# Gate and up zeros: replicated by DMA instead of spread by a one-hot product

## The chip, the cores and the metric

One NeuronCore of a Trainium2 chip runs the whole kernel. It has five engines that run their own queues in order: PE (matrix products), DVE (VectorE), ACT (ScalarE), POOL (GpSimd) and SP (SyncE, which here only issues DMAs). They share SBUF, the on-chip memory of 128 partitions; products land in PSUM, of which each matmul output here takes one bank of 512 float32 per partition. The metric is the time of one execution on the device in microseconds (us). A profiled execution also leaves a trace, whose span begins with the first instruction and ends with the last.

## The reference

x has 1024 rows of 512. After a layer norm two branches are computed from the same xn: an attention with 32 heads (8 key and value heads), and a feed-forward block with quantised weights, whose output, through a SiLU, gates the attention. Only the feed-forward block matters for the change:

```python
def dequantize(imatrix, scales, zeros, group_size, out_dtype):
    rs = jnp.repeat(scales, group_size, axis=0)
    rz = jnp.repeat(zeros, group_size, axis=0)
    return ((imatrix.astype(rs.dtype) - rz.astype(rs.dtype)) * rs).astype(out_dtype)
gate_proj = dequantize(gate_w, gate_s, gate_z, GROUP_SIZE, dt)   # 512 x 1792, groups of 128 rows
up_proj = dequantize(up_w, up_s, up_z, GROUP_SIZE, dt)
down_proj = dequantize(down_w, down_s, down_z, GROUP_SIZE, dt)
gate = jax.nn.silu(jnp.dot(x, gate_proj))
up = jnp.dot(x, up_proj)
return jnp.dot(gate * up, down_proj)
...
x = x + s * g        # s: the attention of xn; g: silu of the feed-forward block of xn
```

Weights and zeros are integers from 0 to 15. A group is 128 input rows, so for each of the 4 groups (KT) every column has one zero and one scale.

## The kernel before

The kernel runs the feed-forward block first and the attention after it. The block's 1792 hidden columns are cut into 14 units (NI) of 128 columns. A unit holds its gate columns (m = 0) and its up columns (m = 1) side by side: integer weights of 128 partitions x 4 groups x 256 columns.

For each unit these steps are taken:

- gu_load (L228) brings the unit's integer weights into one of three buffers (tag "wi"), 512 KB.
- The zeros have to stand in all 128 partitions, since they are the same for all rows of a group. Three ways exist. gu_zeros (L222) once loads the zeros of all units, 14 rows of 1024, converts them to f16 (z16), and makes the one-hot matrices (pick). gu_spread (L237) then makes a unit's zeros in PSUM (z_ps) by two matmuls, each with the one-hot matrix that picks the unit's row and 512 of its columns; z_ps takes one of the four PSUM tiles that the products of the stage rotate through (pair, two banks each). gu_zeros_load (L244) brings them by one DMA that reads the unit's four rows of 256 numbers for each partition, into a row of h that is still free, as integers; units 1 and 2 use it, with the rows NI - 5 + it, that is 10 and 11.
- gu_subtract (L250) takes weights minus zeros on DVE and writes f16 (guq, three buffers). All products of the unit read guq.
- gu_unit (L312) multiplies. xn is held as a sum of two f16 parts (xth, xtl), so each product is two matmuls. Units 0 to 2 are done in two halves of 512 rows (tb = 0, 1), units 3 to 13 in one go (tb is None): for each m and each group j, four matmuls of 512 columns into one pair.
- gu_scaled (L258) takes a pair out of PSUM with the group's scale: groups 0 and 2 by ACT (L273), groups 1 and 3 by DVE, which adds onto what ACT wrote (L275). The two sums that arise are added by POOL (gu_total, L295). The Silu is ACT's (L299), and gate times up goes into the unit's row of h (gu_h, L305): by POOL for odd units, by DVE for even ones and for the halves.

h (L209) is 14 rows of 1024 numbers in each partition; row it belongs to unit it. Rows 12 and 13 first hold half of x (ln_load), rows 10 and 11 the zeros of units 1 and 2.

The order of the work on every engine is written out by hand: instructions stand on each engine in the order of the Python code. A unit's gate and h, which are late, are done in the next unit (gu_finish, lists in behind), after its first group for m = 0 and for m = 1. In the same way unit it, after its first group, prepares unit it + 1: it spreads the zeros (L357; L317 for the halves), subtracts (L358), and issues the weight load of unit it + 4 (L360, gu_load(subtract + 3)), into the buffer that the subtract has just freed. Behind that weight load on SP stands one of the loads of the first projection weights (L803, wide).

Around the stage: ln_* make xth and xtl; unit 10 is followed by a few small products for the first projection (norms, L590 and L595 on DVE), and in units 12 and 13 the first down weights are prepared (dn_dequant L491, whose L493 and L494 are a difference and a product; split_r L143, whose L147 is a difference; all of them with both inputs in SBUF). The down stage (L826) follows, then the attention.

Of the kernel before, what the change touches and what calls it, by code (L numbers as in the profile page):

```python
# [15 lines left out]
I32 = mybir.dt.int32  # L16
# [14 lines left out]
NI = FF // P  # L31
NT = S // P
HT = NT // 2
KT = DM // P
# [75 lines left out]
def attention_gated_by_ffn_kernel(ctx, tc, x, gu_w, gu_z, gu_s, dn_w, dn_z, dn_s, wq, wkv, wo, qnw, knw, out):  # L110
# [98 lines left out]
    h = fp.tile([P, NI, S], F32, name="h")  # L209
# [3 lines left out]
    def pair(name):  # L213
        return fpsum.tile([P, 2, 512], F32, tag="pair", name=name)
# [13 lines left out]
    def gu_load(it):  # L228
        wi = gp.tile([P, KT, 256], I32, tag="wi", name=f"gui{it}", bufs=3)
        if it:  # L230
            sp.dma_start(wi, gu_w[it])
        else:
            for m in range(2):
                sp.dma_start(wi[:, :, m * P : m * P + P], gu_w[it][:, :, m * P : m * P + P])
        gu_raw[it] = wi

    def gu_spread(it):  # L237

        ps = pair(f"z_ps{it}")
        for k in range(2):  # L240
            te.matmul(ps[:, k, :], lhsT=pick[:, it, :], rhs=z16[:, k * 512 : k * 512 + 512], start=True, stop=True)
        gu_raw[it, "z"] = ps.rearrange("p a c -> p (a c)").rearrange("p (k c) -> p k c", k=KT)

    def gu_zeros_load(it):  # L244

        zb = h[:, NI - 5 + it, :].bitcast(I32).rearrange("p (k c) -> p k c", k=KT)
        sp.dma_start(zb, gu_z[:, it].partition_broadcast(P))
        gu_raw[it, "z"] = zb

    def gu_subtract(it, m=None):  # L250
        if it not in gu_int:
            gu_int[it] = gp.tile([P, KT, 256], F16, tag="wq", name=f"guq{it}", bufs=3)
        c = slice(0, 256) if m is None else slice(m * P, m * P + P)
        ve.tensor_tensor(gu_int[it][:, :, c], gu_raw[it][:, :, c], gu_raw[it, "z"][:, :, c], ALU.subtract)
# [3 lines left out]
    def gu_scaled(unit, m, j, ps):  # L258

        it, tb = unit  # L260
        w = ps.shape[1]
        if j == 0:
            if tb is None or m == 0:
                tag = m if tb is None else (it + tb + 1) % 2
                two = gu_sums[unit, "tile"] = gp.tile([P, 2, S], F32, tag=("gs", "us")[tag], name=f"g{m}_{it}_{tb}")
            else:
                two = gu_sums[unit, "tile"][:, :, 512:]
            for i in range(2):
                gu_sums[unit, m, 2 * i] = two[:, i, :w]
        a = gu_sums[unit, m, j - j % 2]  # L270
        scale = gsT[:, it, m, j : j + 1]
        if j % 2 == 0:
            se.activation(a, ps, AF.Copy, scale=scale)  # L273
        else:
            ve.scalar_tensor_tensor(a, ps, scale, a, ALU.mult, ALU.add)  # L275

    def gu_first(m, banks):

        two = gp.tile([P, 2, S], F32, tag=("gs", "us")[m], name=f"g{m}_first")
        parts = [two[:, 0, :512], two[:, 1, :512], two[:, 0, 512:]]  # L280
        for j, a in enumerate(parts):
            se.activation(a, banks[j], AF.Copy, scale=gsT[:, 0, m, j : j + 1])
        gu_sums[(0, 0), m, 0] = parts[0]

        def rest():
            a, b, c = parts
            ve.scalar_tensor_tensor(c, banks[3], gsT[:, 0, m, 3:4], c, ALU.mult, ALU.add)
            ge.tensor_tensor(a, a, b, ALU.add)
            ge.tensor_tensor(a, a, c, ALU.add)

        return rest

    def gu_total(unit, m):
        a = gu_sums[unit, m, 0]
        ge.tensor_tensor(a, a, gu_sums.pop((unit, m, 2)), ALU.add)  # L295
# [11 lines left out]
    def gu_finish(k):  # L307

        if behind[k]:
            (gu_gate, gu_h)[k](behind[k].pop(0))  # L310

    def gu_unit(it, tb, subtract=None, first=False, halfway=lambda rest: None, finish=True, meanwhile=lambda: None, total=True):  # L312
        unit = (it, tb)
        w = gu_int[it]
        rest = []
        if subtract is not None and tb is not None:
            gu_spread(subtract)  # L317
        for m in range(2):
            ws = slice(m * P, m * P + P)
            banks = {}  # L320
            for j in range(KT):
                if tb is None:
                    banks[j] = pair(f"gu_ps{it}_{m}_{j}")
                    for x in (xth, xtl):
                        for k in range(2):
                            te.matmul(
                                banks[j][:, k, :], lhsT=w[:, j, ws], rhs=x[:, j, k * 512 : k * 512 + 512], start=x is xth, stop=x is xtl
                            )
                    banks[j] = banks[j].rearrange("p a c -> p (a c)")
                else:  # L330
                    if j % 2 == 0:
                        both = pair(f"gu_ps{it}_{tb}_{m}_{j}")
                    banks[j] = both[:, j % 2, :]
                    if not (first and m == 0):
                        for x in (xth, xtl):
                            te.matmul(
                                banks[j], lhsT=w[:, j, ws], rhs=x[:, j, tb * 512 : tb * 512 + 512], start=x is xth, stop=x is xtl
                            )
                    elif j == KT - 1:
                        for c in (0, 256):  # L340
                            for x in (xth, xtl):
                                for i in range(KT):
                                    te.matmul(
                                        banks[i][:, c : c + 256], lhsT=w[:, i, ws], rhs=x[:, i, c : c + 256], start=x is xth, stop=x is xtl
                                    )
                if tb is None:
                    gu_scaled(unit, m, j, banks[j])
                elif j % 2 and not first:
                    for i in (j - 1, j):
                        gu_scaled(unit, m, i, banks[i])  # L350
                if j == 0 and finish and tb is None:
                    gu_finish(m)
                    if total and m == 1:
                        gu_total(unit, 0)
                if m == 0 and j == (1 if tb is not None else 0) and subtract is not None:
                    if tb is None:
                        gu_spread(subtract)  # L357
                    gu_subtract(subtract)  # L358
                    if subtract + 3 < NI:
                        gu_load(subtract + 3)  # L360
                if m == 0 and j == 1 and tb is None:
                    meanwhile()
            if first:
                rest.append(gu_first(m, banks))
            elif total and not (tb is None and m == 0):
                gu_total(unit, m)
            for _ in range(finish if tb is not None else 0):
                gu_finish(m)
            if m == 0:
                halfway(rest)  # L370
        for k in range(2):
            behind[k].append(unit)
        return rest
# [53 lines left out]
    for t in range(HT, NT):  # L427
        ln_load(t)
    gu_load(1)
    gu_zeros_load(1)  # L430
    gu_load(2)
    gu_zeros_load(2)

    warm = pair("warm")[:, 0, :]
# [14 lines left out]
        ln_split(t)  # L449
    for it in (3, 4, 5):  # L450
        gu_load(it)

    def other_rows(rest):

        for t in range(HT, NT):
            ln_stats(t)
            if t > HT:
                ln_moments(t - 1)
        ln_moments(NT - 1)
        ln_rstd(1, lambda: gu_subtract(1))  # L460
        for t in range(HT, NT):
            ln_norm(t)
        rest.pop(0)()
        gu_subtract(2)

    for f in gu_unit(0, 0, first=True, finish=False, halfway=other_rows):
        f()
    gu_unit(1, 0, finish=False)
    for t in range(HT, NT):
        ln_transpose(t)  # L470
        ln_split(t)
    gu_unit(2, 0, finish=2)
    gu_unit(0, 1, finish=1)
    gu_unit(1, 1, finish=1)
# [351 lines left out]
    for it in range(NI):  # L826
        for tb in range(2):
# [14 lines left out]
            for i in range(4):  # L842
                c = slice(i * P, i * P + P)
# [529 lines left out]
```

## Time and profile before

| what | us |
|---|---|
| median of three runs | 1022.02 |
| lowest and highest of them | 1018.25, 1023.63 |
| the profiled execution | 1020.44 |
| its span in the trace | 1018.6 |
| PE busy in the span | 964.7 (95%) |
| DVE busy | 857.2 (84%) |
| ACT busy | 775.5 (76%) |
| POOL busy | 429.4 (42%) |
| units 0 to 2 (halves) begin, units 3 to 13 begin, down stage begins | 13.1, 45.2, 130.7 |

Shares over the whole span are means over stages with different limits: POOL, at 42% of the span, is busy for 67 of the 85.5 us of the units 3 to 13. The instructions that make and use the zeros, by the view of the lines:

```profile
L241 PE MATMUL z_ps<-z,pick x24: 374/379/385, 7.9 to 115.3; 14*128 14x512 f16 x24
L254 DVE TENSOR_TENSOR guq<-gui,z_ps x13: 679/1210/1221, 8.5 to 115.8; 128x1024 f16<-128x1024 int32 x11, 128x512 f16<-128x512 int32 x2
```

The columns are line, engine, operation, count, the shortest, middle and longest duration in ns, and the first and last start in us. A matmul's recorded duration is longer than the distance to the next one's start, because matmuls overlap in the array; costs on PE are therefore read from starts.

### The profile page before, as it was taken

How to read it: one execution, taken by the hardware profiler on the slowest of the kernel's cores; microseconds unless marked ns; L12 is line 12 of the kernel's file. 1: busy time of each engine (PE TensorE's matmuls, PEld its weight loads, DVE VectorE, ACT ScalarE, POOL GpSimd, SP SyncE). 2: the span in 40 equal slices, each digit the busy share in tenths (PEclk: the TensorE clock that was granted, in tenths of full speed). 3: DMA queues.
4: the chain of work that ended last, by engine and by line, in shares of the span. 5: the costliest groups of instructions: out<-in, count | busy, mean ns of one | idle time of the engine just before them, and what ended most of it. 6: DMA issues, size and time to landing. Idle time of an engine off the chain costs nothing. (4 is left out here: it accounts for less than half of the span.)

```text
span 1018.6 us, 17980 instructions
## 1 busy us (share of the span) xinstructions
PE 964.7 (95%) x5688; PEld 561.8 (55%) x5688; DVE 857.2 (84%) x1764; ACT 775.5 (76%) x2160; POOL 429.4 (42%) x424
## 2 busy tenths in 40 slices
PE   6899999999999999996998999999999999989995
PEld 4344477854444444444555666665676666656562
DVE  7888998728888878877898998987989989969985
ACT  5777745778878887787887987987879978858861
POOL 2588764216666555564235151051241421530722
PEclk9999999999999999999999999999999999999999
DMA  7132359535998999998898999997999999999994
GB/s 251 37 121 93 104 170 310 187 125 163 204 273 190 245 229 215 236 237 202 172 196 161 206 216 183 227 203 158 231 202 191 212 201 190 202 219 198 218 201 108
DMA packets 425063, 195.74 MB, mean 192 GB/s; under 512 B 371522, under 2 KB 382078, under 8 KB 424958
## 3 DMA queue, kind: packets, MB, share of 16 engines
q1 hardware_dynamic: 424958, 194.50, 85.5%
q8 instruction: 46, 0.75, 0.3%
q14 instruction: 59, 0.48, 0.1%
HBM read 76.27 MB, written 27.27 MB: 102 GB/s over the span
## 5 line engine op out<-in xcount | busy, mean ns | idle before, releaser
L1074 DVE SCALAR_TENSOR_TENSOR p<-pf,row,p 128x384 f16<-128x384 f32 (+7 forms) x256 | 208.8, 816 | 20.9 <-ACT p L1066 18.0
L1047 ACT ACTIVATE pf<-pf,row 128x384 f32<-128x384 f32 (+7 forms) x256 | 184.9, 723 | 41.6 <-DVE row L1041 37.3
L1041 DVE CUSTOM_DVE_ANT_0 pf<-s,trel,cs 128x384 f32<-128x384 f32 (+7 forms) x256 | 191.4, 748 | 19.8 <-PE s L153 19.7
L1066 ACT ACTIVATE p<-pf,row 128x384 f16<-128x384 f32 (+7 forms) x256 | 184.0, 719 | 6.3 <-DMA pT<-p 1.4
L151 PE MATMUL s<-kT,qT 128*128 128x512 f16 (+3 forms) x356 | 115.3, 324 | 11.8 <-DVE row L1041 11.5
L994 POOL TENSOR_SCALAR wl<-wl,rvs 128x512 f32<-128x512 f32 x32 | 53.7, 1677 | 149.0 <-DMA wl<-in_wo 130.0
L152 PE MATMUL s<-kT,qT 128*128 128x512 f16 (+3 forms) x356 | 115.4, 324 | 0.0
L153 PE MATMUL s<-kT,qT 128*128 128x512 f16 (+3 forms) x356 | 114.0, 325 | 0.0
L716 POOL TENSOR_TENSOR f<-f,inv 128x512 f32<-128x512 f32 (+1 forms) x96 | 102.1, 1084 | 1.4
L151 PE MATMUL m<-v,wh 128*128 128x512 f16 x248 | 95.0, 383 | 0.0
L153 PE MATMUL m<-v,wh 128*128 128x512 f16 x248 | 94.9, 383 | 0.0
L151 PE MATMUL o<-pT,vT 128*128 128x256 f16 (+1 forms) x302 | 79.6, 264 | 13.9 <-DMA pT<-p 13.7
L151 PEld LDWEIGHTS <-vT 128*128 128x128 f16 x594 | 58.9, 99 | 57.8 <-DMA pT<-p 15.1
L1110 ACT ACTIVATE wh<-o 128x256 f16<-128x256 f32 x128 | 47.7, 373 | 54.4 <-PE o L153 53.8
L152 PEld LDWEIGHTS <-vT 128*128 128x128 f16 x594 | 58.9, 99 | 41.4 <-issue 4.5
L152 PE MATMUL o<-pT,vT 128*128 128x256 f16 (+1 forms) x302 | 79.6, 264 | 0.0
L153 PE MATMUL o<-pT,vT 128*128 128x256 f16 (+1 forms) x302 | 79.3, 264 | 0.0
L151 PE MATMUL o<-wide,vT 128*128 128x256 f16 (+1 forms) x292 | 75.9, 260 | 3.1 <-DMA wide<-p 3.1
L152 PE MATMUL o<-wide,vT 128*128 128x256 f16 (+1 forms) x292 | 75.9, 260 | 0.0
L153 PE MATMUL o<-wide,vT 128*128 128x256 f16 (+1 forms) x292 | 75.7, 260 | 0.0
L151 PE MATMUL m<-wh,xth 128*128 128x512 f16 x192 | 72.8, 379 | 1.2 <-ACT h L869 1.2
L153 PE MATMUL m<-wh,xtl 128*128 128x512 f16 x192 | 72.8, 379 | 0.0
(200 smaller groups left out, 2531.4 us busy)
## 6 DMA issues: line engine op xcount, KB each, us to landing
qd<-tr SPq DMA_DIRECT2D x48, 256.0 KB, 3.3
qT<-qd SPq DMA_DIRECT2D x24, 512.0 KB, 4.4
wide<-in_wq SPq DMA_DIRECT2D x32, 256.0 KB, 3.7
wo_sq<-in_wo SPq DMA_DIRECT2D x8, 1024.0 KB, 7.8
wl<-in_wo SPq DMA_DIRECT2D x32, 256.0 KB, 3.6
gui<-in_gu_w SPq DMA_DIRECT2D x13, 512.0 KB, 3.7
wide<-in_wkv SPq DMA_DIRECT2D x16, 256.0 KB, 3.8
vd<-v SPq DMA_DIRECT2D x8, 512.0 KB, 4.7
```

The lines of the kernel that those rows point to most:

```text
L151: te.matmul(ps, lhsT=lh, rhs=rh, start=first, stop=False)
L152: te.matmul(ps, lhsT=lh, rhs=rl, start=False, stop=False)
L153: te.matmul(ps, lhsT=ll, rhs=rh, start=False, stop=last)
L716: ge.tensor_tensor(f, f, ib, ALU.mult)
L994: ge.tensor_scalar(wor[g, i], wor[g, i], rvs[:, g : g + 1], None, ALU.mult)
L1041: ve.tensor_tensor_reduce(p, ps, trel[g][:, S - w :], cs[:, hh : hh + 1], 3e38, ALU.add, ALU.min, least[:, c])
L1047: se.activation(p, p, AF.Exp, bias=least[:, c], scale=-1.0, accum_out=total[:, c])
L1066: se.activation(p16[u, qt][:, :, 0, :], pf[u, qt], AF.Copy, scale=scale[:, qt : qt + 1])
L1074: ve.scalar_tensor_tensor(lo, p, scale, hi, ALU.mult, ALU.subtract)
L1110: se.activation(oh, av_ps[u], AF.Copy, scale=1.0 / P_SCALE)
```

## The change

The zeros of units 3 to 13 no longer come from products. gu_zeros_load now serves every unit but the first, into the unit's own row of h from unit 3 on, and the spreads in gu_unit go. The loads for units 3 to 5 stand behind their weight loads at the beginning, those for units 6 to 13 behind the weight load of the same unit. gu_subtract is the same line as before, but its second input, for units 3 to 13, is h in SBUF in place of z_ps in PSUM. Unit 0 keeps its spread.

```diff
     def gu_zeros_load(it):
 
-        zb = h[:, NI - 5 + it, :].bitcast(I32).rearrange("p (k c) -> p k c", k=KT)
+        row = NI - 5 + it if it < 3 else it
+        zb = h[:, row, :].bitcast(I32).rearrange("p (k c) -> p k c", k=KT)
         sp.dma_start(zb, gu_z[:, it].partition_broadcast(P))
         gu_raw[it, "z"] = zb
...
         rest = []
-        if subtract is not None and tb is not None:
-            gu_spread(subtract)
         for m in range(2):
...
                 if m == 0 and j == (1 if tb is not None else 0) and subtract is not None:
-                    if tb is None:
-                        gu_spread(subtract)
                     gu_subtract(subtract)
                     if subtract + 3 < NI:
                         gu_load(subtract + 3)
+                        gu_zeros_load(subtract + 3)
...
     for it in (3, 4, 5):
         gu_load(it)
+        gu_zeros_load(it)
```

## The prediction

> **What bounds the kernel now.** I read three views, in this order: the busy time of the engines over the gate and up stage (its units 3 to 13 run from 45.2 to 130.7 us), the timeline of one pair of units in it, and the timeline wherever VectorE (DVE) and GpSimd (POOL) meet.
>
> ```profile
> core 0: us, PE busy (x) PEld busy (x) DVE busy (x) ACT busy (x) POOL busy (x), PEclk, DMA share, GB/s
> 45.20:130.70 85.50, 83.56 (x378) 35.02 (x378) 77.55 (x69) 61.90 (x64) 67.08 (x28) 1.00 0.33 106
> ```
>
> Of 85.5 us PE is busy 83.6, DVE 77.6 and POOL 67.1: PE sets the pace, at full clock (1.00), and DVE stands only 10% behind. DMA is busy a third of the time.
>
> ```profile
> 60.76 0.59 PE L326 MATMUL gu_ps<-xtl,guq 128*128 128x512 f16 x2
> 61.29 0.60 PE L241 MATMUL z_ps<-z,pick 14*128 14x512 f16 x2
> 61.82 0.61 PE L326 MATMUL gu_ps<-xth,guq 128*128 128x512 f16 x2
> ```
>
> Columns, here and below: start, duration, engine, line, operation. This is PE around one spread, L241. The spreads of units 4, 5 and 6 start at 53.74, 61.29 and 68.83: a unit takes 7.55 us, a pair 15.09, and PE has no gap in between. The other two engines in the same pair:
>
> ```profile
> 54.63 2.36 POOL L295 TENSOR_TENSOR g_None<-g_None 128x1024 f32<-128x1024 f32 x1 [0.50 <-DVE g_None L275]
> 57.07 2.36 POOL L305 TENSOR_TENSOR h<-g_None 128x1024 f32<-128x1024 f32 x1
> 59.40 2.35 POOL L295 TENSOR_TENSOR g_None<-g_None 128x1024 f32<-128x1024 f32 x1
> 62.18 2.37 POOL L295 TENSOR_TENSOR g_None<-g_None 128x1024 f32<-128x1024 f32 x1 [0.43 <-DVE g_None L275]
> 66.34 3.21 POOL L295 TENSOR_TENSOR g_None<-g_None 128x1024 f32<-128x1024 f32 x1 [1.79 <-DVE g_None L275]
> ```
>
> ```profile
> 62.02 1.21 DVE L254 TENSOR_TENSOR guq<-gui,z_ps 128x1024 f16<-128x1024 int32 x1
> ...
> 66.11 1.22 DVE L305 TENSOR_TENSOR h<-g_None 128x1024 f32<-128x1024 f32 x1
> ```
>
> An even unit (4, from 54.47, its subtract, on) has three POOL instructions: the second total of the unit before (L295), an odd unit's h (L305), its own first total (L295). An odd unit (5, from 62.02 on) has two, and DVE makes the even unit's h (66.11). POOL's L295 takes 2.37 us beside the subtract L254, but 3.21 us beside DVE's h.
>
> ```profile
> 21.44 1.22 DVE L254 TENSOR_TENSOR guq<-gui,h 128x1024 f16<-128x1024 int32 x1
> ...
> 21.67 2.11 POOL L289 TENSOR_TENSOR g_first<-g_first 128x512 f32<-128x512 f32 x1 [3.75 <-DVE g_first L287]
> ...
> 118.42 2.68 POOL L305 TENSOR_TENSOR h<-g_None 128x1024 f32<-128x1024 f32 x1
> ...
> 118.93 2.72 DVE L494 TENSOR_TENSOR dni<-dni,dns 128x512 f32<-128x512 f32 x1
> ...
> 138.45 1.11 DVE L147 TENSOR_TENSOR dnl<-dni,dnh 128x512 fp32r<-128x512 f32 x1 [1.84 <-ACT dnh L145]
> ...
> 138.97 2.85 POOL L295 TENSOR_TENSOR g_None<-g_None 128x1024 f32<-128x1024 f32 x1
> ```
>
> The first two rows are the future form of the subtract, with zeros from h in SBUF (units 1 and 2 have it already): POOL's 512-wide sum, 1.28 us two rows later (23.73), takes 2.11, because it gets going only when the subtract is over (22.66). The next two are the reverse: a DVE product of two SBUF tiles (this width takes 0.68 us undisturbed, as at 144.02) ends at 121.65, 0.55 after POOL's h (121.10). So a DVE instruction with both inputs in SBUF and a POOL instruction exclude each other, and the one that comes second waits for the other's end. With one input in PSUM they don't: beside the subtract at 62.02 POOL kept its 2.37. The last two show who comes next when both wait: a POOL instruction ended at 139.01 with the next one ready, and DVE's 138.45 still ended at 139.56, 0.55 after the first, while POOL's next was stretched to 2.85. DVE gets in between.
>
> **What the change removes.** Eleven spreads (L241, two matmuls and two weight loads each). The price of one: the group before it starts its last pair at 60.76, the next group would start 0.43 later, at 61.19, and starts at 61.82: 0.63 us. Eleven are 6.9 us of PE, and PE's pair would fall from 15.09 to 13.83. It also takes z_ps out of the four PSUM pairs, which lets PE run a pair further ahead.
>
> **What it adds on the queues.** Eleven loads of 512 KB through SP, each some 0.65 us to issue (this load's own rows for units 1 and 2: 0.66 and 0.63). They stand behind the weight load of the same unit and ahead of a wide<-in_wkv or wide<-in_wq load, which then goes out 0.65 later and is read first at 98.4. The zeros of unit 6 go out near 45.6 and are read at 62.0. This load's own two landings took 8.3 and 9.3 us (in the first 20 us, where the DMA share is 0.80; in the stage it is 0.33), so some 7 us of cover are left; I take 0. Without the cover a late landing would hold DVE's subtract and, one unit later, PE, by what it is late. The rows of h that are used are written by their own unit much later and wait for nothing.
>
> **What it moves: the subtract onto POOL's port.** Its duration stays (1.21 with z_ps, 1.21 to 1.22 with h). But it now excludes POOL, ten times in this stretch. I work out a pair by hand from the rows. A DVE 1024-wide instruction that has waited ends 1.08 after POOL's end (1.21 less the 0.13 by which the 512-wide 0.68 exceeds 0.55). A POOL 1024-wide one that has waited ends 2.22 after DVE's end (66.34+3.21 against 66.11+1.22). DVE starts its next instruction 1.13 after a subtract, 1.2 after an L275.
>
> Even unit, from its subtract at 0, which starts 0.16 ahead of POOL's total as at 62.02 and 62.18: subtract to 1.21, POOL's second total to 3.43, h to 5.87 (back to back, 2.44 as 57.07 to 59.40 and neighbours), first total to 8.19. DVE meanwhile needs only 1.13 and four times L275: it wants its next subtract at about 6.8 and finds POOL in flight until 8.19. That subtract ends at 9.27, as if it had started at 8.06. Even unit: 8.06.
>
> Odd unit, from there: subtract to 1.21, POOL's total to 3.43. DVE: L275 at 1.13, a second at 2.4 (ScalarE's Silu had to wait for the total that ended 0.13 into the unit), DVE's h at 3.6 to 4.84, POOL's first total waits and ends at 7.06, L275 at 4.75 and 5.94, next subtract at 7.12, just after POOL is through. Odd unit: 7.12.
>
> The pair: 15.18 against 15.09 now. Put as a sum: five POOL instructions of 2.36 (11.8) and three DVE ones of 1.08 that exclude them (3.25) are 15.05, and POOL now has no idle time left to pay with. So what PE gives up is taken by the port between DVE and POOL; five pairs cost +0.5 instead of -6.3.
>
> The edges: the unit 2 subtract at 43.96 meets a POOL sum that ends at 44.31: +0.23, given back by the spread that went before it. In unit 11 two small DVE reads (L590, L595) stand ahead of the subtract, so that POOL's total (now ready at about 108.05, after an h that waits for Silu as now) goes first and the subtract ends at 111.5 instead of 109.3; the next one is at 117.3 instead of 115.8. In unit 12 the wait of L494 (2.04 of its 2.72) is given back: L493 and L494 follow each other while POOL is held, and the L275 behind them starts at 121.85 against 121.57. At 126.7 L147 finds POOL's last total in flight until 128.8 (now 127.66). The down stage begins 1.1 us later than 130.67. From there PE is busy (19.9 of 20 us in 140 to 160) and the shift goes through to the end. **Sum:** +1.2 us; bounds of the unknown part -6.9 (the exclusion costs nothing) and +11.5 (below). On the profiled execution, 1020.44 us with a span of 1018.6, that is 1021.6; the median of the three runs is 1022.02, so the forecast is 1023.2.
>
> One rule of the Trainium skill speaks for the opposite: Perfetto Trace Analysis, Optimization Strategies, makes it the goal to keep the matmul engine used and to work on whatever blocks it. By it, 6.9 us taken off a PE that waits for nobody would be 6.9 us gained, a time of 1015.1, against 1023.2 by the rows; the rows at 21.44 and 21.67 are why I don't follow it.
>
> **Rivals.** (1) PE stays the bound and the 6.9 us come out: 1015.1. For it: POOL is idle 2.4 us a pair today, DVE 1.8, PE not at all. Against it: the pair would have to shrink by 1.26 and hold two more exclusions of 1.08, which is 3.4 us out of POOL's 2.4. (2) The port goes to the wrong one: when the even unit's first total ends, POOL's second total, long ready, goes ahead of the waiting subtract (8.19 to 10.53). DVE's subtract, and with it h and the rest of the odd unit, comes 2.3 later: the pair is 17.5, five pairs +11.5, 1033.5. It decides above 0.5% from three pairs of five on (2.3 x 3 = 6.9). Against it is 138.45 to 139.56; for it, that the margin by which the subtract leads POOL's total elsewhere is only 0.16 us, which unit 11 loses. (3) The zeros land late, or the change moves no PE time at all: the first needs a landing over 16 us, the second is excluded by the 22 matmuls that the built program no longer has.
>
> **Chances.** What a measurement of this kernel can tell from no change is about 0.5%, 5.1 us. The forecast (a change between -4 and +5 us): 0.60. Rival 1, or most of it: 0.10. Beyond +5: 0.30, half of it rival 2 at most pairs, half single lost margins of about 2 us each, three or more of them. So faster 0.10, same 0.60, slower 0.30. The forecast's own range is 1019 to 1027; to leave out no more than two in ten I take 1018 to 1030.
>
> **What would show it.** Right: L254 stands at 1.2 in some units and 2 to 3 us in others, alternating; POOL's L295 mean rises from 2.55 to about 3; PE shows waits for DVE of about 1.3 us a pair where it had 0.63 of spread; pairs of subtracts stay 15.1 to 15.2 apart. Wrong: pairs of 13.9 (rival 1), or of 17.5 with DVE waiting through two POOL instructions (rival 2). A first matmul of a unit that waits for a DMA of in_gu_z would be rival 3.

## The result and the profile after

| | us |
|---|---|
| changed kernel, median of 22 runs | 1022.68 (1018.8 to 1026.4) |
| kernel before, median of 22 runs beside them | 1019.87 (1015.03 to 1023.63) |
| ratio of the two | 1.0031, 95% interval 1.0018 to 1.0044 |
| profiled execution of the changed kernel, and its span | 1018.8, 1016.9 |
| first and last start of a matmul of the down stage, before | 130.67, 208.81 |
| the same, changed | 133.77, 211.63 |

By the ratio, the change made the kernel slower by about 3.2 us (1.8 to 4.5), which lies inside the 0.5% that the forecast counted as no change. The predicted 1023.2 lies 0.5 from the measured 1022.68, but part of that is luck: the kernel before measured 1019.87 beside it and not the 1022.02 that the forecast started from. To be compared with the forecast's +1.2 is the +3.2. The profiled execution of the changed kernel is the quickest of its 22 runs, and the one of the kernel before is slower than its median; so the two traces are compared interval by interval and not by their spans.

Line numbers of the changed kernel are one higher than before's from the subtract (L255) to h (L306): L276 is DVE's accumulation, L274 ACT's copy, L296 POOL's total, L300 the Silu. First the engines in units 3 to 13, in the kernel before and in the changed one (busy us and, in brackets, instructions of PE, PEld, DVE, ACT and POOL, then clock, DMA share and GB/s):

```profile
core 0: us, PE busy (x) PEld busy (x) DVE busy (x) ACT busy (x) POOL busy (x), PEclk, DMA share, GB/s
45.00:131.00 86.00, 83.98 (x379) 35.28 (x379) 78.05 (x70) 62.40 (x66) 67.15 (x28) 1.00 0.33 106
...
45.00:131.00 86.00, 77.00 (x355) 34.36 (x354) 82.85 (x67) 60.61 (x65) 75.25 (x28) 1.00 0.46 153
```

PE lost the 7 us of the spreads, as the change meant it to, and DVE went from 78.05 to 82.85 of 86 us, POOL from 67.15 to 75.25. The waits of the same stretch (total us, times, longest) tell who is waited for, first a row of the kernel before, then the same of the changed one:

```profile
PE gu_ps L326 <- DVE g_None L275: 1.5, 3, 1.1
...
PE gu_ps L325 <- DVE g_None L276: 7.5, 6, 3.0
```

PE's waits for DVE's accumulations were 1.5 us before and are 7.5 now: the time that the spreads left went there, 6.0 of it. Now one pair of units (start, duration, engine, line, operation). A subtract stands one unit ahead of the unit whose weights it makes: "unit 3's subtract" makes unit 3's weights and stands in unit 2; "the even unit's subtract" stands in an even unit.

```profile
72.42 1.21 DVE L255 TENSOR_TENSOR guq<-gui,h 128x1024 f16<-128x1024 int32 x1
72.58 3.28 POOL L296 TENSOR_TENSOR g_None<-g_None 128x1024 f32<-128x1024 f32 x1 [0.24 <-DVE g_None L276]
...
78.25 5.65 POOL L296 TENSOR_TENSOR g_None<-g_None 128x1024 f32<-128x1024 f32 x2
...
79.02 2.66 DVE L255 TENSOR_TENSOR guq<-gui,h 128x1024 f16<-128x1024 int32 x1
...
83.99 1.21 DVE L306 TENSOR_TENSOR h<-g_None 128x1024 f32<-128x1024 f32 x1
...
87.51 1.21 DVE L255 TENSOR_TENSOR guq<-gui,h 128x1024 f16<-128x1024 int32 x1
```

The even unit's subtract (72.42) goes first, and POOL's total beside it, 2.37 in the kernel before, takes 3.28. The odd unit's subtract (79.02) finds POOL in flight, takes 2.66, and stretches the two totals of POOL's row at 78.25 to 5.65 (4.7 without it). From 72.42 to 87.51 the pair is 15.09, what it was before (15.16, 15.09 and 15.10), and so are its neighbours (57.33, 72.42, 87.51, 102.60). The pairs gained nothing and lost nothing. What the trace shows as lost lies at the two ends of the stage. Its start, in the kernel before and in the changed one:

```profile
43.96 1.21 DVE L254 TENSOR_TENSOR guq<-gui,z_ps 128x1024 f16<-128x1024 int32 x1
...
54.47 1.21 DVE L254 TENSOR_TENSOR guq<-gui,z_ps 128x1024 f16<-128x1024 int32 x1
```

```profile
43.16 2.95 POOL L296 TENSOR_TENSOR g<-g 128x512 f32<-128x512 f32 x2 [0.33 <-DVE g L276]
...
45.56 1.64 DVE L255 TENSOR_TENSOR guq<-gui,h 128x1024 f16<-128x1024 int32 x1
...
48.00 2.95 POOL L296 TENSOR_TENSOR g<-g 128x512 f32<-128x512 f32 x2 [1.89 <-DVE g L276]
...
49.75 2.29 DVE L255 TENSOR_TENSOR guq<-gui,h 128x1024 f16<-128x1024 int32 x1
...
57.33 1.21 DVE L255 TENSOR_TENSOR guq<-gui,h 128x1024 f16<-128x1024 int32 x1
```

The subtracts of units 3 and 4 (45.56, 49.75), which took 1.21 before, take 1.64 and 2.29, each behind one of POOL's 512-wide totals. The stage's end, again before and changed:

```profile
118.14 0.75 DVE L493 TENSOR_TENSOR dni<-dni,dnz 128x512 f32<-128x512 int32 x1
...
122.90 0.59 PE L326 MATMUL gu_ps<-xth,guq 128*128 128x512 f16 x2 [1.12 <-DVE g_None L275]
```

```profile
108.42 5.67 POOL L296 TENSOR_TENSOR g_None<-g_None 128x1024 f32<-128x1024 f32 x2
...
110.66 1.22 DVE L255 TENSOR_TENSOR guq<-gui,h 128x1024 f16<-128x1024 int32 x1
...
118.18 3.27 POOL L296 TENSOR_TENSOR g_None<-g_None 128x1024 f32<-128x1024 f32 x1 [0.24 <-DVE g_None L276]
...
120.35 1.66 DVE L492 TENSOR_TENSOR dni<-dni,dnz 128x512 f32<-128x512 int32 x1
...
121.53 2.68 POOL L306 TENSOR_TENSOR h<-g_None 128x1024 f32<-128x1024 f32 x1
122.04 2.71 DVE L493 TENSOR_TENSOR dni<-dni,dns 128x512 f32<-128x512 f32 x1
...
126.00 0.59 PE L325 MATMUL gu_ps<-xth,guq 128*128 128x512 f16 x2 [2.95 <-DVE g_None L276]
```

In unit 11 the subtract (110.66, unit 12's) kept its 1.22. In unit 12 the first down-weight subtract (120.35), which was 0.75 before, finds POOL's stretched total of 118.18 in flight and takes 1.66, and DVE's next one still waits for POOL's h (121.53), as before. The accumulations behind them are late by that much, and PE waits 2.95 us for one of them where it waited 1.12.

Read from these two executions, interval by interval:

| interval | before | changed | difference |
|---|---|---|---|
| unit 3's subtract to unit 5's | 10.51 | 11.77 | +1.26 |
| unit 5's to unit 11's | 45.35 | 45.27 | -0.08 |
| unit 11's to unit 13's | 16.00 | 15.42 | -0.58 |
| unit 13's to the first matmul of the down stage | 14.85 | 15.75 | +0.90 |
| sum | 86.71 | 88.21 | +1.50 |

The other 1.6 of the 3.1 us that the table shows at the down stage's start were there ahead of unit 3's subtract (45.56 against 43.96). I put them down to this execution and not to the change: its granted clock over the first 43 us is 0.92 where before's is 1.00, two windows of 3.4 us in which PE had half its clock, and the first of them began at 12.1, ahead of the first load that the change adds (13.16). Three kernels below had two such windows there as well (45.53, 44.73 and, with the second window twice as long, 46.91; the first of the three has none of the added loads); in those without a window this subtract stands at 43.8 to 44.6, with the loads or without.

### The profile page after: what moved, and what is told of

Same layout as the page of the kernel before. It is cut to its first block, busy times and chain, and to the rows that moved or that the text cites. A ratio compares the mean times of both kernels' runs of the same rounds, so it can differ in the third digit from the quotient of the medians.

```text
span 1016.9 us, 17949 instructions
## 1 busy us (share of the span) xinstructions
PE 955.1 (94%) x5666; PEld 559.7 (55%) x5666; DVE 862.1 (85%) x1764; ACT 774.6 (76%) x2160; POOL 436.5 (43%) x424
## 5 line engine op out<-in xcount | busy, mean ns | idle before, releaser
L1073 DVE SCALAR_TENSOR_TENSOR p<-pf,row,p 128x384 f16<-128x384 f32 (+7 forms) x256 | 206.5, 806 | 22.9 <-ACT p L1065 19.8
L153 PE MATMUL o<-wh,xtl 128*128 128x512 f16 x192 | 72.8, 379 | 0.0
```

The costliest lines, as they stand in the source:

```text
L153: te.matmul(ps, lhsT=ll, rhs=rh, start=False, stop=last)
L1073: ve.scalar_tensor_tensor(lo, p, scale, hi, ALU.mult, ALU.subtract)
```

## The experiments

Four questions: does the exclusion of DVE and POOL set the pair, do the loads cost anything, is it the exclusion alone, and where does the loss come from. Every ratio is to runs of the kernel before, taken beside it.

**The subtract with its second input in PSUM.** The loads stay, but the subtract of units 3 to 13 reads a product's PSUM pair in place of the zeros, and compares instead of subtracting; the zeros are left out, and the kernel's values mean nothing:

```diff
-        ve.tensor_tensor(gu_int[it][:, :, c], gu_raw[it][:, :, c], gu_raw[it, "z"][:, :, c], ALU.subtract)
+        ve.tensor_tensor(gu_int[it], gu_raw[it], from_psum.rearrange("p (k c) -> p k c", k=KT), ALU.is_gt)
```

> The changed kernel with the loads of the zeros kept, but the subtract of units 3 to 13 reads a PSUM pair (the unit's first product) as its second input in place of h; it leaves out the zeros (it compares with the product, so the values mean nothing). Theory (DVE and POOL exclude each other when the subtract has two SBUF inputs, and that takes what PE gave up): the subtract no longer holds POOL up, POOL's sums beside it are back at 2.36 us, pairs of units fall from 15.09 to about 13.9, the time is 5 to 7 us below the kernel before: 0.9935 to 0.995 of it, some 1013.5. Rival (the loads by DMA or the other PSUM slots take it): pairs stay at 15.1, the time stays near 1.003 of the kernel before.

Measured: 1016.48, ratio 0.9983 (0.9966 to 1.0000). The pairs:

```profile
68.94 1.21 DVE L258 TENSOR_TENSOR guq<-gui,gu_ps 128x1024 f16<-128x1024 int32 x1
69.10 2.37 POOL L299 TENSOR_TENSOR g_None<-g_None 128x1024 f32<-128x1024 f32 x1 [0.24 <-DVE g_None L279]
...
75.92 1.22 DVE L258 TENSOR_TENSOR guq<-gui,gu_ps 128x1024 f16<-128x1024 int32 x1 [0.50 <-ACT g_None L277]
...
83.21 1.22 DVE L258 TENSOR_TENSOR guq<-gui,gu_ps 128x1024 f16<-128x1024 int32 x1
```

68.94 to 83.21 is 14.27 (the one before it 14.04), and POOL's total beside the subtract is back at 2.37. So a DVE instruction in the same place, with the same duration and the same number of elements, costs the pair 0.8 to 1.05 us less when one input is not in SBUF. The total gained less than the expected 0.9935 to 0.995: this instruction also waits for ACT to have read that pair (some 0.5 in most units; 1.78 in unit 10, where the third pair becomes 15.9).

**The spreads put back, unread.** All eleven stand again where they stood, and nobody reads z_ps:

```diff
+                    if tb is None:
+                        gu_spread(subtract, False)
                     gu_subtract(subtract)
```

> The changed kernel with all eleven spreads put back on PE, unread; the subtract still reads h. Theory: PE's pair is 15.09 again, the pair of DVE and POOL is 15.09 too, so the time is that of the changed kernel or up to 2 us more: 1.003 to 1.005 of the kernel before. Rival (the spreads' 6.9 us of PE were really gained, and something else costs 10 us): 6.9 us above the changed kernel, 1.010 of the kernel before.

Measured: 1020.49, ratio 1.0013 (0.9996 to 1.0031): under the expected 1.003 to 1.005, and not slower than the changed kernel (1.0018 to 1.0044).

```profile
70.97 1.21 DVE L256 TENSOR_TENSOR guq<-gui,h 128x1024 f16<-128x1024 int32 x1
...
78.21 2.03 DVE L256 TENSOR_TENSOR guq<-gui,h 128x1024 f16<-128x1024 int32 x1
...
86.07 1.21 DVE L256 TENSOR_TENSOR guq<-gui,h 128x1024 f16<-128x1024 int32 x1
```

The pair is 15.10 with 1.26 us more of PE work in it. PE had that time to spare: what the change took off PE was worth nothing.

**POOL relieved, in the changed kernel and in the one before.** The product gate times up of the odd units from 3 on is left out; ACT writes the gate into h.

```diff
+        if tb is None and it % 2:
+            se.activation(h[:, it, :], a, AF.Silu)
+            return
         se.activation(a, a, AF.Silu)
```

> The changed kernel, with the product of gate and up left out for the odd units of 3 to 13 (ScalarE writes the gate alone into h), so that POOL has 2.36 us less per pair. Theory: POOL and the exclusion need 12.7 us a pair, PE 13.83: PE is the bound again, pairs about 13.9, the time 5 to 7 us below the changed kernel, 0.996 to 0.999 of the kernel before. Rival (the pair is not made of POOL's time): pairs stay at 15.1 and the time at 1.003.

> The kernel before with the same product left out. Theory: PE is the bound of the pair there, POOL's 2.36 us less are worth nothing, pairs stay at 15.09: 0.999 to 1.001 of the kernel before. Rival (POOL's length counts in both kernels): 4 us or more faster.

Measured: 1018.21, ratio 1.0003 (0.9982 to 1.0024) for the changed kernel, 1018.64, ratio 1.0005 (0.9986 to 1.0024) for the one before. The pairs answer: 13.59, 13.81 and 13.82 in the first, 15.15, 15.10 and 15.09 in the second. With one POOL instruction less, the changed kernel reaches PE's own pair (15.09 less two spreads of 0.63 is 13.83); the kernel before gains nothing from it. The total of the first did not follow: 0.996 to 0.999 was expected. In its profile the 3.0 us that it led at the down stage's first matmul (127.64) were gone at the last one (208.78); both kernels had a half-clock window in that stage there, which took 81.14 and 81.16 us against 78.14 before. Whether that is so in its other runs is not shown. It had also lost 1.7 us in unit 11:

```profile
104.58 2.36 POOL L296 TENSOR_TENSOR g_None<-g_None 128x1024 f32<-128x1024 f32 x1 [0.16 <-DVE g_None L276]
104.75 3.27 DVE L255 TENSOR_TENSOR guq<-gui,h 128x1024 f16<-128x1024 int32 x1
...
113.85 1.21 DVE L255 TENSOR_TENSOR guq<-gui,h 128x1024 f16<-128x1024 int32 x1
```

Here POOL's total went 0.17 ahead of the subtract, which took 3.27, and the next subtract came 9.10 us after it (7.36 in the changed kernel). This is the loss that the forecast had put into unit 11 of the changed kernel; there the subtract (110.66) came when the first of two POOL totals was about to end, and took 1.22.

**The loads alone.** The kernel before with the eleven loads, which nobody reads:

```diff
                         gu_load(subtract + 3)
+                        gu_zeros_load(subtract + 3)
```

> The kernel before, plus the eleven zeros loads of the change, issued at the change's place and read by nobody; the subtract keeps z_ps. My theory costs the loads at nothing: pairs of 15.09 to 15.1, subtracts at 1.21, first matmul of the down stage at 130.5 to 131 with no half-clock window in between, ratio 0.999 to 1.001. Rival (the loads, through SP's queue or the DMA engines, carry the 3 us of the change): first matmul of the down stage or the time after it later by 2 to 3 us, ratio 1.002 to 1.004.

Measured: 1017.43, ratio 1.0002 (0.9985 to 1.0019); pairs 15.16, 15.09, 15.09, subtracts at 1.21, the down stage from 130.56. The loads cost nothing that shows.

**One exclusion a pair instead of two.** Zeros by DMA for the odd units 5 to 13 (their subtracts stand in even units, where DVE goes first), by spread for the others:

```diff
+                    if spread and tb is None:
+                        gu_spread(subtract)
                     gu_subtract(subtract)
                     if subtract + 3 < NI:
                         gu_load(subtract + 3)
-                        gu_zeros_load(subtract + 3)
+                        if subtract + 3 > 3 and subtract + 3 % 2:
+                            gu_zeros_load(subtract + 3)
```

The last condition reads subtract + (3 % 2) and so holds for every unit: the zeros of units 6, 8, 10 and 12 were loaded as well, and nobody read them (the trace has 11 such loads, with those of units 1 and 2). The run before this one has eleven unread loads, and nothing is longer by them.

> The zeros of units 5, 7, 9, 11 and 13 come by DMA, those of 3, 4, 6, 8, 10 and 12 by spread. The subtract from SBUF then stands only in even units, where it already went ahead of POOL at 1.2 us in the changed kernel (57.33, 72.42, 87.51, 102.60, 118.02). Exclusion theory: POOL's pair is 5 x 2.36 + 2 x 1.08 = 13.96 us, less than PE's 13.83 + 0.63 = 14.46, so PE is the bound again: pairs of subtracts 14.4 to 14.5 apart against 15.09, four pairs -2.5, unit 13 up to -0.6 more, no collision at units 3 and 4: first matmul of the down stage about 127.6 to 128.2 with no half-clock window in between (130.67 before), total about -2.5 us (-1 to -3), ratio 0.997. Rival (every pair that holds one exclusion more stays at 15.1, or POOL's queued work goes ahead): pairs of 15.1 or more, ratio 1.000 or above.

Measured: 1019.44, ratio 1.0022 (0.9998 to 1.0047). This one fell:

```profile
70.04 1.22 DVE L255 TENSOR_TENSOR guq<-gui,h 128x1024 f16<-128x1024 int32 x1
70.21 3.28 POOL L296 TENSOR_TENSOR g_None<-g_None 128x1024 f32<-128x1024 f32 x1 [0.24 <-DVE g_None L276]
...
75.88 4.67 POOL L296 TENSOR_TENSOR g_None<-g_None 128x1024 f32<-128x1024 f32 x2
...
76.38 1.21 DVE L255 TENSOR_TENSOR guq<-gui,z_ps 128x1024 f16<-128x1024 int32 x1
...
78.27 1.06 ACT L300 ACTIVATE g_None<-g_None 128x1024 f32<-128x1024 f32 x1 [1.20 <-POOL g_None L296]
79.23 2.10 ACT L274 ACTIVATE g_None<-gu_ps,gsT 128x1024 f32<-128x1024 f32 x2
80.36 1.28 DVE L276 SCALAR_TENSOR_TENSOR g_None<-gu_ps,gsT,g_None 128x1024 f32<-128x1024 f32 x1 [1.57 <-ACT g_None L274]
...
85.08 1.22 DVE L255 TENSOR_TENSOR guq<-gui,h 128x1024 f16<-128x1024 int32 x1
```

The odd unit's subtract (76.38, from z_ps) waits for nobody, POOL is busy for 13.47 us of the pair, PE needs 14.46 (13.83 and one spread of 0.63), and the pair is still 15.04. So adding up the port is not enough. The rows show a loop of dependences instead, and no wait for a DMA in it. From 70.04 on, POOL's three queued instructions end at 78.27, 8.23 later (0.9 of it from the one exclusion: 3.28 instead of 2.37). The last of them releases the Silu (78.27, which waited 1.20 for it). ACT's next copy stands behind the Silu, 0.96 later, and DVE's accumulation (80.36) waits 1.57 for that copy, 1.13 after it began. DVE then has an accumulation, h and two more accumulations without a gap (1.20, 1.13, 2.39) until the next subtract. 8.23 + 0.96 + 1.13 + 1.20 + 1.13 + 2.39 = 15.04.

**The loop broken.** Zeros by DMA for units 5, 7, 9 and 11, and in these units the Silu is issued behind the copy of the third group. Against the kernel above this also leaves out the four unread loads, and unit 13 is spread again, behind the pairs read here. No run has the later Silu beside the unread loads; that these are not what held the pair rests on the run with the loads alone and on the rows above. A control has the later Silu in the kernel before; a third kernel has it with the zeros of units 5 to 12 by DMA.

```diff
-                if j == 0 and finish and tb is None:
+                if j == (2 if m == 0 and it in (5, 7, 9, 11) else 0) and finish and tb is None:
                     gu_finish(m)
```

> Zeros by DMA for units 5, 7, 9 and 11 only, and in units 5, 7, 9 and 11 ScalarE issues its Silu after the copy of the third group (j = 2) of the same unit in place of ahead of it. Theory from the run with the odd units' zeros by DMA (pairs of 15.04 although only one exclusion is left and PE needs 14.46): the exclusion puts POOL's three queued instructions 1.08 later, the last of them releases Silu at 8.23 after the pair's start, ScalarE's next copy stands behind Silu, and DVE's rest of the unit behind that: 8.23 + 0.96 + 1.13 + 1.20 + 1.13 + 2.39 = 15.04. With Silu behind that copy the loop is broken and PE decides: pairs of subtracts (unit 5 to 7, 7 to 9, 9 to 11) 14.4 to 14.5 apart, first matmul of the down stage 2 to 2.5 us ahead of before's 130.67 if no half-clock window falls in between, ratio 0.996 to 0.999. If the pairs stay at 15.04, the loop does not run through Silu.

> Control: the kernel before with the same later Silu in units 5, 7, 9 and 11. PE sets its pace, so nothing changes: pairs 15.09, first matmul of the down stage at 130.7 with no half-clock window in between, ratio 0.999 to 1.001.

> Zeros by DMA for units 5 to 12 (3, 4 and 13 by spread), and the later Silu. Here the odd unit's subtract also waits for POOL (until 8.06 after the pair's start) and DVE then has 7.03 us of instructions without a gap, so the loop through Silu is not the only one: pairs stay 15.0 to 15.1. Against the run with units 5 to 13 by DMA, unit 13's spread gives back the wait of the first down-weight subtract (1.66 again 0.75 us): first matmul of the down stage up to 0.9 earlier, ratio to before 0.998 to 1.000. If pairs fall to 14.5, the exclusion of the odd unit's subtract was no bound of its own.

The first, pair and engines (columns as in the table of engines above):

```profile
69.51 1.22 DVE L255 TENSOR_TENSOR guq<-gui,h 128x1024 f16<-128x1024 int32 x1
...
78.09 1.11 ACT L274 ACTIVATE g_None<-gu_ps,gsT 128x1024 f32<-128x1024 f32 x1 [1.19 <-PE gu_ps L328]
79.10 1.05 ACT L300 ACTIVATE g_None<-g_None 128x1024 f32<-128x1024 f32 x1
79.24 1.28 DVE L276 SCALAR_TENSOR_TENSOR g_None<-gu_ps,gsT,g_None 128x1024 f32<-128x1024 f32 x1 [0.48 <-ACT g_None L274]
...
83.96 1.22 DVE L255 TENSOR_TENSOR guq<-gui,h 128x1024 f16<-128x1024 int32 x1
```

```profile
54.00:98.00 44.00, 44.00 (x203) 19.15 (x202) 40.48 (x34) 32.64 (x33) 40.79 (x16) 1.00 0.38 135
```

The copy (78.09) is ahead of the Silu (79.10), DVE's accumulation starts at 79.24, and the pairs are 14.52, 14.45 and 14.45: PE's 14.46, with PE busy 44.00 of 44.00. The control has 15.16, 15.09 and 15.10 and a ratio of 1.0000 (0.9982 to 1.0017). In the third kernel the later Silu brings nothing, as expected:

```profile
69.42 1.21 DVE L255 TENSOR_TENSOR guq<-gui,h 128x1024 f16<-128x1024 int32 x1
...
75.75 2.95 DVE L255 TENSOR_TENSOR guq<-gui,h 128x1024 f16<-128x1024 int32 x1
...
84.52 1.21 DVE L255 TENSOR_TENSOR guq<-gui,h 128x1024 f16<-128x1024 int32 x1
```

Its pairs are 15.11, 15.10 and 15.10: with the odd unit's subtract excluded too (75.75, 2.95), DVE has no gap from that subtract's end to the next, and this second loop is as long as the first. So the changed kernel, whose rows show both, stands on two loops of 15.0 to 15.1, and both start at the exclusion.

Total: 1016.86, ratio 0.9993 (0.9975 to 1.0011) for the first, against an expected 0.996 to 0.999; 1017.85, ratio 1.0005 (0.9990 to 1.0020) for the third, against 0.998 to 1.000. From unit 3's subtract to the down stage the first is 1.9 us shorter than before (84.81 against 86.71). That is the shortest stage found with nothing left out, but its whole time can't be told from that of the kernel before; where the 1.9 us went was not tried.

**Where the loss is.** Units 3 and 4 put back to spreads, and, the other way round, the change made for units 3 and 4 alone:

```diff
+        spread = subtract is not None and not (subtract > 4)
```

```diff
+        spread = subtract is not None and not (subtract in (3, 4))
```

> The changed kernel with units 3 and 4 put back to spreads (z_ps), units 5 to 13 by DMA. If the collisions of unit 3's and unit 4's subtract with POOL's 512-wide totals (1.64 and 2.29 instead of 1.21) are what the changed kernel loses at the start of the stage, the subtracts stand at 43.9 and 47.7 at 1.2 us again, unit 5's at 54.5 to 55.5 instead of 57.33, pairs stay 15.09, and the total is 1.0 to 2.0 us under the changed kernel: ratio to the kernel before 1.001 to 1.002. Rival (the start costs nothing that stays, the loss is at units 11 to 13 or later): ratio 1.003 as the changed kernel.

> The kernel before with the change made for units 3 and 4 alone (5 to 13 keep their spreads). If the part of the changed kernel's loss that I did not forecast sits at the collisions of these two subtracts with POOL's 512-wide totals, the subtracts take 1.6 and 2.3 us here too, unit 5's subtract comes 11.8 after unit 3's instead of 10.5, the pairs behind it stay at 15.1 and the first matmul of the down stage is 1.3 us later than before's 130.67 (with no half-clock window ahead of it), ratio 1.001 to 1.002. If the loss is elsewhere, these two units cost nothing (PE saves 2 x 0.63 here) and the ratio is 1.000 or below. A ratio of 1.003 or more would put the whole of it here.

Measured: 1016.84, ratio 0.9992 (0.9972 to 1.0012) without the change in these two units; 1018.27, ratio 1.0018 (0.9997 to 1.0038) with it there alone. The second is as expected; the first is under its 1.001 to 1.002, that is, more is gone from the time than these two subtracts cost in the trace. In the second:

```profile
44.73 1.63 DVE L255 TENSOR_TENSOR guq<-gui,h 128x1024 f16<-128x1024 int32 x1
...
48.91 2.29 DVE L255 TENSOR_TENSOR guq<-gui,h 128x1024 f16<-128x1024 int32 x1
...
56.49 1.20 DVE L255 TENSOR_TENSOR guq<-gui,z_ps 128x1024 f16<-128x1024 int32 x1
```

From unit 3's subtract to unit 5's it is 11.76, as in the changed kernel (11.77); with the spreads kept there it is 10.51, as before. Behind it the second kernel won back 0.6 at once (unit 6's subtract comes 6.91 after unit 5's, 7.55 before), which I read, untested, as PE catching up on a wait; the changed kernel's pairs leave no room for that. The last 0.9 stands with unit 13: from its subtract to the down stage it takes 15.75 and 15.76 us in the changed kernel and with the odd units' zeros by DMA, which both load unit 13's zeros, and 14.85 to 14.88 in the kernel before, the loads alone, the three with the later Silu and the change in 3 and 4 alone, which all spread them.

One more thing stands at that place. PE's longest wait behind unit 13's subtract, 1.12 us before and 2.95 in the changed kernel, is 2.0 or more in six of the traced kernels, all with a changed subtract of unit 13, and in three of these (PSUM operand, spreads put back, units 3 and 4 by spread) a window at half clock begins in that wait or at most 1.3 us after it; in the eight kernels where it is 1.62 or less there is none. In the last two of the three the way from unit 13's subtract to the down stage is 16.51 and 17.61 us in place of 15.75. The profiled execution of the changed kernel had no window there. So a window behind the longer wait is a candidate for what is missing between the trace and the 22 runs, but it is not shown: over the whole span these runs lost 11.2 us of clock on average (span times what the mean clock is short of 1), the kernel before 9.7 to 11.4 in the runs beside the experiments.

**A try at a faster version.** Units 3 and 4 by spread, 5 to 13 by DMA; even units add up m = 1 in one chain on DVE without POOL's total, and POOL makes every h:

```diff
+        chain = tb is None and m == 1 and it % 2 == 0
-        a = gu_sums[unit, m, j - j % 2]
+        a = gu_sums[unit, m, 0 if chain else j - j % 2]
...
-        engine = ge if tb is None and it % 2 else ve
+        engine = ge if tb is None else ve
```

> As the run before (units 3, 4 by spread, 5 to 13 by DMA), and the port is relieved without leaving work out: in even units the second accumulation (m = 1) is a chain of one ScalarE and three DVE instructions in one tile, with no POOL total, and every unit's h is POOL's. Exclusion theory: a pair then has five POOL instructions (11.8) and two DVE ones that exclude them (2 x 1.08), 13.96 us, beside PE's 13.83 and DVE's 9 x 1.19 + 2 x 1.13 = 13.0: pairs of 14.0 to 14.4 instead of 15.09, total -2 to -4 us against the kernel before, ratio 0.996 to 0.998. If DVE's waits for POOL add to its 13.0 in full (2 x 1.08 or more), pairs of 15 or above and nothing is won.

Measured: 1020.03, ratio 1.0029 (1.0008 to 1.0049). The pairs did fall, to 14.60 to 14.62, but from unit 11's subtract to unit 12's it now takes 9.86 us (8.30 before), and the down stage, first to last matmul, 79.5 (78.1); 0.996 to 0.998 was expected. Why that stage is longer was not tried.

## Why the prediction was right, and where not

- **The spreads' price and what is left of it.** 0.63 each and 6.9 in all came off PE, and nothing of it off the time: shown by the windows and by the spreads put back.
- **The exclusion fills the pair.** 15.18 by hand, 15.09 measured, with subtracts of 1.2 and 2.7 to 2.9 us in turn, as named. The walk put the end of the odd unit's subtract at 9.27 after the even one's start; it ended at 9.26 (72.42 to 81.68). Its "2.44 as 57.07 to 59.40" is misread (these rows are 2.33 apart; 54.63 to 57.07 is 2.44), without effect on that end. The PSUM operand (first two pairs 14.04 and 14.27) and the relieved POOL (13.6 to 13.8) show that it is the exclusion, whose price per POOL total is 0.9 us (3.28 instead of 2.37). But the sentence that POOL then "has no idle time left to pay with" is wrong as it stands: the sum took 1.08 per exclusion off POOL, it was 0.9 to 0.95 (3.28 for 2.37, 5.65 for 4.7) at the two subtracts, and POOL was busy for 14.45 us of the pair's 15.09; with one exclusion, 13.47 us of POOL and PE at 14.46 the pair was still 15.04. The step by step walk through the pair had the Silu's wait in it; the sum over the port had not, and it was the sum that I then trusted to size a better version.
- **Queue and loads at 0.** Right: 1.0002 (0.9985 to 1.0019). In the changed kernel such a load takes 4.8 us from issue to landing (median), and no subtract of units 3 to 13 waits for one; with that rival 3 fell too.
- **The edges, +1.1 at the down stage.** +1.5 measured, from other places. "The unit 2 subtract at 43.96 meets a POOL sum", +0.23: measured +0.43. The next one, unit 4's, was not in the forecast and took +1.08: that is the term that failed, by leaving one collision out, since there too a POOL total was in flight. Of the two, 0.25 was given back by unit 5's subtract (+1.26). Unit 11's loss didn't occur: -0.58 there, where the forecast has the next subtract 1.5 later in all, some 0.5 of it from the pairs; the mechanism exists, as the run with POOL relieved showed. Unit 12's give-back didn't occur: instead of two DVE instructions in a row, POOL's h got in between, as it had in the kernel before (118.42, ahead of 118.93); its wait stayed (2.71, 2.72 before), and the first DVE instruction now waits too (1.66, 0.75 before), which is the +0.9.
- **The sum.** +1.2 forecast, +3.2 measured (1.8 to 4.5), +1.5 found in the trace. The rest, 0.3 to 3.0 us by the interval, stays open. The down stage itself is not longer in these traces (78.14 before, 77.86 now), and the two kernels that hold half of the change each, 0.9992 and 1.0018, leave it open too. That the forecast's 1023.2 came so near is owed to this: a start 2.2 us too high and a loss 2.0 us too small.
- **Rival 1, PE stays the bound (1015.1).** Fell: pairs of 15.09. The rule behind it, which the Trainium skill gives on Perfetto Trace Analysis, Optimization Strategies, is to keep the matmul engine used and to work on what blocks it; PE was used 83.98 of 86 us before, and taking work off it left it used 77.00 of 86 in the same time.
- **Rival 2, POOL's queued work goes first (1033.5).** Fell at the pairs: DVE got in between each time. The 0.16 us by which DVE leads is as thin as feared: where it was lost once (104.58 against 104.75, POOL relieved) the next subtract came 9.10 us later and not 7.36.

## What to carry to other kernels

When an engine is relieved, look for what the relief moves into: here a DVE instruction changed its second input from PSUM to SBUF, kept its 1.21 us wherever it came first, and cost POOL 0.9 us each time, and the 6.9 us of saved PE time were gone. Adding up a shared resource gave only a lower bound here (13.96 by the sum, 15.04 measured); the time was set by the longest closed chain through the queues (POOL, Silu, ACT's copy, DVE, next subtract), and such a chain is written down by following who releases whom for one period. Where a chain was the bound, moving one instruction on a third engine took 0.6 us off a pair (15.04 to 14.45), and removing PE's work took off nothing; in the whole time of the kernel neither showed a gain.

## What the runs showed of the hardware that was not expected

- Three POOL instructions in a row and one DVE instruction with two SBUF inputs: DVE got its turn at the first boundary between two POOL instructions in each pair of the changed kernel (the row at 78.25); POOL got its turn between two such DVE instructions as well (POOL's h at 121.53, between DVE's 120.35 and 122.04), where the forecast had DVE keep it.
- Windows of 3.4 us (twice that in two executions) at half clock stand in some executions and not in others. In the first 215 us of the fourteen traces each of them begins in a pause of PE of 1.18 us or more or at most 1.5 us after its end (in the changed kernel PE pauses from 8.38 to 10.85, and the first window begins at 12.1); pauses of that length stand without a window too (the 2.95 us at 126.00). With two of 3.4 us ahead of unit 3, its subtract stood at 44.73 to 45.56 in place of 43.8 to 44.6. In the 22 runs of the changed kernel the span is longer by about 0.5 us for each us of clock lost (correlation 0.66).
